# A planned Trainium2 kernel: other durations in its plan, four graph pairs in flight for five, and one output transfer for each graph

## The chip, the cores and the metric

The program runs on one core of one Trainium2 chip. The metric is the device time of one execution in microseconds, and less is better. Three runs of the kernel before took 3004.53, 3000.09 and 3002.74 us, a median of 3002.74 us.

## What is computed

The input is 64 graphs of 256 nodes with 256 features and a 0/1 adjacency of 256 x 256, all in float32. Two layers follow each other. Layer 0 is a graph attention layer used twice in a row, a layernorm, and a feed-forward block with ReLU. Layer 1 is an attention with 8 heads of 32 features, in which adjacency values pick the value projection, a layernorm, and a feed-forward block with GELU.

```python
# layer 0
def _gat(h, adj, W, a, out_features):
    Wh = jnp.matmul(h, W)
    e = leaky_relu(Wh @ a[:out_features] + swapaxes(Wh @ a[out_features:], 1, 2), 0.2)
    att = softmax(where(adj > 0, e, NEG), axis=1)
    return jnp.matmul(att, Wh)
h = _gat(_gat(x, adj, W1, a1), adj, W2, a2)
h = _layernorm(x + h)
x = _layernorm(h + relu(h @ w_ff1 + b_ff1) @ w_ff2 + b_ff2)
# layer 1
scores = einsum('bhid,bhjd->bhij', q, k) / sqrt(dh)
attn = softmax(scores, axis=-1)
for r in range(R):                       # adj holds 0 and 1 here
    out = out + einsum('bhij,bhjd->bhid', attn * (adj == r)[:, None], v_r)
x = _ln(src + out.reshape(Bb, Nn, Dm) @ Wo + bo)
return _ln(x + gelu(x @ W1 + b1) @ W2 + b2)
```

## The kernel before

The work goes by pairs of graphs, 32 of them, numbered 0 to 31 here. For each pair the generator `whole_way` gives the matmul steps of all its stages: `gat_layers` (first, second and third GAT product, "GAT1" to "GAT3" below), `feed_forward` of layer 0, `attention`, `feed_forward` of layer 1, and the store of the rows. A step is a handful of matmuls; in front of each the generator yields what the step needs: events, an exclusive name, and a number of PSUM banks. The other engines' work, the DMAs too, is handed over with `put(engine, us, emit, *events, rank=...)`.

The order of the instructions on every engine is settled before anything runs, by `run`. It is a list scheduler with a clock for each engine. `took(us)` moves TensorE's clock by a duration that is written in the code, and `put` carries one for its piece. At each turn `run` takes the engine that can begin first. On TensorE it chooses among the steps that have been ready for `SLACK` (0.3 us) the one of the lowest degree, then the one of the oldest pair. The degree is 0 for the pair in the first half of a feed-forward, 2 for a pair in its second half (`filling`), and 1 else. On another engine it takes the piece of the lowest rank. The order in which `run` emits is the order in which each engine executes on the chip; there the engines wait on semaphores alone, so that the durations in the code change the order and nothing else.

Some things are exclusive. Only one pair at a time holds the name "gat" (GAT1 and GAT2), only one "ff" (a feed-forward from its first product to its last), only one "attention" (from the first q/k/v product to the output projection). There are 4 buffers for a pair's rows `x`, 4 for its adjacency in bytes `adj`, one `input` buffer for the adjacency and the transposed input in turn, two `yT` for transposed rows, and 8 PSUM banks. `whole_way` asks for the loads of the next pair when it begins.

How many pairs are in flight is the last argument of `run`, called `together`. `run` adds 1 to it for the weights' own generator `reliefs`, which leaves after the start. In the kernel before that line stands twice:

```python
        going, ways = [[besides, *next(besides)]], iter(ways)
        together += 1
        ...
        together += 1
        while True:
            while len(going) < together and (way := next(ways, None)) is not None:
                going.append([way, *next(way)])
```

With `run(reliefs(), ..., 4)` five pairs are in flight. A new pair enters when the oldest generator has ended, which is at the last matmul step of its second feed-forward.

TensorE works in two shapes. Nearly all products are made by strips of 32 columns, four matmuls side by side (128 rows x 32 columns, by `by_strips`, line 113, and lines 960 and 963 in `products`). The four `scores` steps of a pair (line 929) contract over 32 rows and are made in the other shape, 32 rows x 128 columns. The steps of the attention stand in this order: the products for q, k and v with scores 0 and 1 among them (`b_.p4`, scores 0, `b_.p3`, scores 1), then products 0, scores 2, products 1, scores 3, products 2, products 3, and the output projection `into_rows`.

`layernorm` centres rows on VectorE (line 654) and scales them there (line 657). `transposed` brings rows into `yT` by a 32 x 32 transposition on VectorE, a store to DRAM (`home`, line 683) and four gathers for each graph (line 689), all on the queue of SyncE. The finished rows of a pair are stored by one transfer of 512 KB on the same queue (line 1097).

Of the kernel before, what the change touches and what calls it, by code (L numbers as in the profile page):

```python
# [18 lines left out]
P = 128  # L19
# [8 lines left out]
SEVEN = ()  # L28
SLACK = 0.3
START = {"tensor": 8.5, "vector": 8.0, "scalar": 4.0, "gpsimd": 0.0, "sync": 32.0}  # L30
# [3 lines left out]
def two_layers(ctx: ExitStack, tc: tile.TileContext, t: dict, out: bass.AP, flag: bass.AP):  # L34
# [114 lines left out]
    alone, filling = {}, []  # L149
# [81 lines left out]
    def run(besides, ways, together):  # L231

        going, ways = [[besides, *next(besides)]], iter(ways)
        together += 1
        def degree(g):
            if g[0] in filling:
                return 2
            return 0 if "ff" in (g[2] or ()) or alone.get("ff") is g[0] else 1  # L240

        together += 1
        while True:
            while len(going) < together and (way := next(ways, None)) is not None:
                going.append([way, *next(way)])
            first = []
            for engine, pieces in waiting.items():
                times = [(at, n) for n, p in enumerate(pieces) if (at := begins(p["ready"], p["needs"])) is not None]
                if times:
                    first.append((max(min(times)[0], clock[engine]), engine, times))  # L250
            times = []
            for n, (way, events, name, banks, *more) in enumerate(going):
                if all(alone.get(n) in (None, way) for n in name or ()) and all(e.time is not None for e in events):
                    at = begins(max([e.time for e in events], default=0.0), "bank" if banks else None, banks)
                    for needs in more:
                        at = None if at is None else begins(at, needs)
                    if at is not None:
                        times.append((at, n))
            if times:
                first.append((max(min(times)[0], clock["tensor"]), "tensor", times))  # L260
            if not first:
                assert not going
                return
            now, engine, times = min(first)
            able = [n for at, n in times if at <= now]
            clock[engine] = now
            if engine == "tensor":
                sure = [n for at, n in times if at <= now - SLACK]
                g = going[min(sure, key=lambda n: (going[n][0] is besides, degree(going[n]), n))
                          if sure else min(times)[1]]  # L270
                alone.update((name, g[0]) for name in g[2] or ())
                takes("bank", g[3])
                for needs in g[4:]:
                    takes(needs)
                step = next(g[0], None)
                if step is None:
                    together -= g[0] is besides
                    going.remove(g)
                else:
                    g[1:] = step  # L280
            else:
                piece = waiting[engine].pop(min(able, key=lambda n: (waiting[engine][n]["rank"], waiting[engine][n]["first"]["ready"])))
                takes(piece["needs"])
                if piece["function"] and piece["function"] != table[0]:
                    table[0] = piece["function"]
                    clock[engine] += 1.3
                piece["emit"]()
                clock[engine] += piece["us"]
                end = clock[engine] + piece["lag"]
                if piece["kb"]:  # L290
                    moved[0] = max(moved[0], clock[engine]) + piece["kb"] / 380.0
                    end = moved[0] + piece["lag"]
                frees_at(end, piece["frees"])
                happens(piece["event"], end)
            keep_order()
# [8 lines left out]
    def load(pair, at=None):  # L304
# [29 lines left out]
        def in_bytes(there):  # L334
            return put("vector", 1.35, largest, put("scalar", 1.2, small_adj, there, needs="adj", rank=2), rank=2)
# [51 lines left out]
    class Second:  # L387


        def __init__(self, b, name, *events):  # L390
            self.b, self.name, self.there, self.read = b, name, [], []
            for n in range(3):
                self.there.append(put("vector", 0.34, lambda n=n: self.add(n), *events, rank=0, needs=None if n else name))
# [10 lines left out]
        def read_by_second(self, event):  # L404
            self.read.append(event)
            if len(self.read) == 2:
                put("vector", 0.34, lambda: self.add(3), self.there[2], *self.read, rank=0, event=self.there[3])
# [7 lines left out]
    class Blocks:  # L415
# [17 lines left out]
        def add(self, c, h, bank, *events, frees=()):  # L433
            def add():
                nc.vector.tensor_tensor(self.target(c, h), self.bank[bank], self.target(c, h), ALU.add)  # L435
            there = put("vector", 0.6, add, *events, rank=-1, frees=frees)
# [41 lines left out]
    def addends(y, there, at, layer, pair):  # L478
# [20 lines left out]
        there = put("scalar", 0.6, exps, *there, rank=0, function="exp")  # L499
# [28 lines left out]
        there = put("vector", 0.2, turn, there, rank=0)  # L528
# [3 lines left out]
    def gat_weights(y, at, at_home, ratio, there, to, b):  # L532
# [20 lines left out]
        there = put("vector", 0.95, lambda: weigh(0), *there, rank=b / 2, needs="e")  # L553
        there = put("vector", 1.13, lambda: weigh(1), there, rank=b / 2, frees=["rows"] * b)
        return of, put_each("scalar", 0.4, [lambda j=j: scale(j) for j in range(2)], there, rank=0)

    def gat_layers(pair, to, loads):
# [3 lines left out]
        def evacuated(to, k, wide, ps):  # L561
            return put("scalar", 0.3, lambda: nc.scalar.activation(to[:, k, :wide], ps[:, :wide], AF.Copy),
                       took(0.88), frees=["bank"])
# [45 lines left out]
    def add_rows(y, p, b, *events):  # L609
# [12 lines left out]
        return of, put_each("vector", 0.44, [lambda j=j: add(j) for j in range(2)], *events, frees=["bank"])  # L622

    def means(y, b, *events):
# [8 lines left out]
        return of, put_each("scalar", 0.54, [lambda j=j: mean(j) for j in range(2)], *events)  # L633

    def layernorm(r, gb, b, added, *events):
# [23 lines left out]
        there = put_each("scalar", 0.54, [lambda j=j: square(j) for j in range(2)], there, rank=0)  # L659
        centred = put_each("vector", 0.34, [lambda j=j: centre(j) for j in range(2)], there)  # L660
        there = put("gpsimd", 1.2, root, there, rank=0)
        return put_each("vector", 0.34, [lambda j=j: scale(j) for j in range(2)], there, centred, *events)
# [5 lines left out]
    def transposed(y, ready, to, b, pair, stage):  # L668
# [23 lines left out]
        there = put("vector", 0.62, turn, ready, needs="yb")  # L692
# [25 lines left out]
    def feed_forward(y, normal, w, func, relieved, gb, pair, stage):  # L718
# [11 lines left out]
        def slabs(t):  # L730
# [11 lines left out]
            def copy(c, h, event):  # L742
                return put("scalar", 0.5, lambda: nc.scalar.activation(target(c, h), blocks.bank["x"], AF.Copy), event, rank=-1)  # L743

            def activate(c, h, event, of=None, frees=()):
                for n in range(2):
# [3 lines left out]
                        to, source, func, bias=b1[:, m:m + 1]), event, rank=h - 1, function=kind,  # L750
# [9 lines left out]
        for step in (a.p1, b.p1, a.p2, a.p6, b.p2, b.p6, a.p5, a.p7, b.p7, b.p5, a.p4, b.p4, a.p3):  # L760
            yield from step()
# [28 lines left out]
    def by_seven(y, normal, f, evacuated, w2, w2_there, last):  # L790
# [21 lines left out]
        def add(to, of, us, *events, frees=()):  # L812
            return put("vector", us, lambda: nc.vector.tensor_tensor(to, of, to, ALU.add), *events, rank=-1, frees=frees)

        def combine(to, a, b, op, *events):
            return put("vector", 1.14, lambda: nc.vector.tensor_tensor(to, a, b, op), *events, rank=0)
# [40 lines left out]
    def attention(y, normal, pair, all_adj):  # L857
# [13 lines left out]
        there = put("scalar", 0.52, lambda: in_one_piece(0), normal[0], needs="yTa")  # L871
        there = put("scalar", 0.52, lambda: in_one_piece(1), there, normal[1], frees=["yT"])
# [27 lines left out]
        def with_bias_qk(c, b, event, frees=()):  # L900
            def copy(n):
                nc.scalar.activation(target_qk(c, b)[:, n], of_qk.bank["x"][:, n], AF.Identity, bias=bqk[:, n, c:c + 1])  # L902
            return [put("scalar", 0.4, lambda n=n: copy(n), event, rank=-1, frees=list(frees) * n) for n in range(2)][1]

        def with_bias_v(r, b, event, frees=()):
# [3 lines left out]
            return put("vector", 0.6, copy, event, rank=-1, frees=frees)  # L909
# [11 lines left out]
        def scores(n):  # L921
            b, c = divmod(n, KC)
            yield [ready["qk", c, b]], None, HQ
# [7 lines left out]
            there = took(1.13)  # L931
# [12 lines left out]
            def halves(q):  # L944
# [3 lines left out]
            there = [put_each("scalar", 0.48, [lambda q=q, k=k: weight(q, k) for k in range(2)], there, rank=0, function="exp",  # L948
                              needs="a", frees=["bank"] * 2) for q in range(HQ // 2)]
            masked.append([put("vector", 1.14, lambda q=q: mask(q), there[q], rank=0, needs="m") for q in range(HQ // 2)] +  # L950
                          [put("vector", 0.61, lambda q=q: halves(q), there[q], rank=0, needs="h") for q in range(HQ // 2)])

        def products(n):
# [10 lines left out]
            there = took(2.34)  # L964
# [16 lines left out]
            there = put("vector", 1.3, invert, there, rank=0)  # L981
            put("scalar", 0.4, check, there, rank=3)
            return put("vector", 0.34, lambda: nc.vector.tensor_tensor(to, po[:, :N], s, ALU.mult), there, rank=0, frees=["bank", "h"])
# [10 lines left out]
        a_, b_ = of_qk, of_v  # L994
        for step in (a_.p1, b_.p1, a_.p2, a_.p6, b_.p2, a_.p5, b_.p6, a_.p7, b_.p5, a_.p4, b_.p7, a_.p3, b_.p4, lambda: scores(0), b_.p3, lambda: scores(1)):
            yield from step()
        frees_at(clock["tensor"], ["yTa", "sums_yTa"])
        divided = []
        for n in range(4):
            yield [*masked[n], ready["v", 0, n // 2], ready["v", 1, n // 2]], None, 1  # L1000
            divided.append(products(n))
            if n < 2:
                yield from scores(n + 2)
# [85 lines left out]
    def whole_way(pair):  # L1089
        to, loads = loaded.pop(pair)  # L1090
        if pair + 1 < NPAIR and pair + 1 not in loaded:
# [5 lines left out]
        put("sync", 0.4, lambda: nc.sync.dma_start(  # L1097
            out[2 * pair:2 * pair + 2].rearrange("b (c p) d -> p (b c) d", p=P), to["x"]),
            normal[0], normal[1], rank=2, lag=1.8, kb=512, frees=["x"])

    run(reliefs(), (whole_way(pair) for pair in range(NPAIR)), 4)


# [442 lines left out]
```

## Time and profile before

| | |
|---|---|
| runs of the kernel | 3004.53, 3000.09, 3002.74 us |
| median | 3002.74 us |
| the profiled execution's own time | 3002.45 us |
| its span (first to last instruction) | 3000.6 us |
| granted TensorE clock, mean | 0.996 |
| TensorE busy | 2962.5 us |
| VectorE busy | 2308.1 us |
| ScalarE busy | 1789.2 us |
| GpSimd busy | 293.3 us |
| DMA queue of SyncE, share of 16 engines | 21.2% |

In the profile PE is TensorE's matmul, PEld its weight load, DVE VectorE, ACT ScalarE, POOL GpSimd, SP SyncE and SPq its queue of issues. `L113` is line 113 of the kernel. A line of the timeline gives the start and the length in us, the engine, the source line, the operation, `out<-in` by the program's names, the tile shape as rows*columns, and how many records are merged. A float32 matmul leaves two records, so that four matmuls side by side over 256 columns are 8 records. The modelled end of a matmul lies after the start of the next one, so that durations of steps are read here from start to start.

### The profile page before, as it was taken

To read this page: it belongs to the slowest core of one execution; us is meant where nothing else is said; L and a number is where in the kernel's file an instruction comes from. 1 tells how busy PE (TensorE), PEld (TensorE's weight loads), DVE (VectorE), ACT (ScalarE), POOL (GpSimd) and SP (SyncE) were. 2 spreads that over 40 slices of the span, in tenths; PEclk is the share of its full clock that TensorE was granted. 3 is DMA by queue.
4 is the path that set the end of the run, shared out by engine and by line. 5 is a ranking of instruction groups with operands and counts; after the bars stand their busy time and mean duration, and the time that the engine had idled before them with its cause. 6 is when DMAs were issued, how large, how long until landed. Compare 5 with 4: busy or idle time off the path is not lost. (4 is left out here: it accounts for less than half of the span.)

```text
span 3000.6 us, 122479 instructions
## 1 busy us (share of the span) xinstructions
PE 2962.5 (99%) x53778; PEld 1766.1 (59%) x53778; DVE 2308.1 (77%) x5865; ACT 1789.2 (60%) x4644; POOL 293.3 (10%) x518
## 2 busy tenths in 40 slices
PE   7999999999999999999999999999999999999998
PEld 4655555555555555555555555555556555565665
DVE  5787875888668887588976888768886788867775
ACT  4555565665656566556665566555666565664554
POOL 0000010000101011000110001101010001100001
PEclk8999999999999999999999999999999999999999
DMA  5221231112321123121231212311232121321100
GB/s 178 80 72 52 65 110 63 52 59 66 108 65 55 55 72 119 52 69 38 92 103 55 62 51 89 99 52 59 65 97 76 59 65 53 100 74 49 39 10 24
DMA packets 211420, 210.22 MB, mean 70 GB/s; under 512 B 22336, under 2 KB 170432, under 8 KB 210880
## 3 DMA queue, kind: packets, MB, share of 16 engines
q1 hardware_dynamic: 210464, 202.06, 21.2%
q8 instruction: 424, 6.95, 1.0%
q14 instruction: 116, 0.95, 0.1%
q10 hardware_dynamic: 416, 0.26, 0.0%
HBM read 137.51 MB, written 64.73 MB: 67 GB/s over the span
## 5 line engine op out<-in xcount | busy, mean ns | idle before, releaser
L113 PE MATMUL ps<-w_L_gnn_W,ff 128*32 128x256 f32 x8192 | 470.7, 380 | 1.3 <-ACT ff L749 1.3
L113 PE MATMUL ps<-w_L_gnn_w_ff,ff 128*32 128x256 f32 x8192 | 470.7, 379 | 0.0
L113 PEld LDWEIGHTS ps<-w_L_gnn_W,ff 128*32 128x32 f32 x8192 | 260.1, 110 | 186.5 <-issue 13.6
L113 PEld LDWEIGHTS ps<-w_L_gnn_w_ff,ff 128*32 128x32 f32 x8192 | 265.1, 110 | 177.5 <-issue 3.6
L938 ACT ACTIVATE a<-ps 128x512 f32<-128x512 f32 x512 | 265.5, 600 | 170.3 <-PE ps L929 153.4
L435 DVE TENSOR_TENSOR ff<-ps,ff 128x512 f32<-128x512 f32 x384 | 262.3, 684 | 118.1 <-PE ps L113 89.6
L650 POOL TENSOR_SCALAR rstd<-squares 128x2 f32<-128x2 f32 x256 | 90.8, 355 | 2679.6 <-ACT unread L645 2678.3
L645 ACT ACTIVATE unread<-x,less 128x256 f32<-128x256 f32 x512 | 259.3, 506 | 130.1 <-DVE less L620 103.7
L942 DVE TENSOR_TENSOR m<-a,adj 128x1024 f32<-128x1024 f32 x256 | 310.7, 1214 | 23.9 <-ACT a L938 23.0
L113 PE MATMUL ps<-yT,w_L_gnn_W1p 128*32 128x256 f32 x5120 | 310.0, 379 | 0.8 <-ACT ff L743 0.3
L113 PE MATMUL ps<-yT,w_L_gnn_w_ff1p 128*32 128x256 f32 x5120 | 306.7, 379 | 0.0
L617 DVE SCALAR_TENSOR_TENSOR x<-ps,x 128x256 f32<-128x256 f32 x512 | 197.3, 417 | 136.0 <-PE ps L113 133.0
L743 ACT ACTIVATE ff<-ps 128x512 f32<-128x512 f32 x384 | 224.2, 588 | 112.9 <-PE ps L113 111.3
L113 PE MATMUL ps<-xw,e 128*32 128x258 f32 (+1 forms) x4096 | 242.7, 386 | 11.9 <-ACT xw L551 11.9
L551 ACT ACTIVATE xw<-xw,rs 128x258 f32<-128x258 f32 (+1 forms) x256 | 118.0, 504 | 201.2 <-DVE rs L547 201.1
L113 PEld LDWEIGHTS ps<-yT,w_L_gnn_W1p 128*32 128x32 f32 x5120 | 165.6, 110 | 112.9 <-ACT ff L743 4.9
L113 PEld LDWEIGHTS ps<-yT,w_L_gnn_w_ff1p 128*32 128x32 f32 x5120 | 165.5, 110 | 110.9 <-issue 2.3
L902 ACT ACTIVATE qk<-ps,bqk 128x256 f32<-128x256 f32 x256 | 107.1, 469 | 190.0 <-PE ps L113 189.8
L749 ACT ACTIVATE ff<-ff,c_L_gnn_b_ff 128x256 f32<-128x256 f32 x384 | 175.5, 503 | 50.5 <-DVE ff L435 47.8
L651 POOL TENSOR_TENSOR rstd<-rstd,mhalf 128x2 f32<-128x2 f32 x256 | 201.8, 788 | 21.3
L113 PEld LDWEIGHTS ps<-xw,e 128*32 128x32 f32 x4096 | 133.8, 112 | 104.6 <-ACT xw L551 14.1
L749 ACT ACTIVATE ff<-ff,c_L_gnn_b 128x256 f32<-128x256 f32 x384 | 175.9, 502 | 28.6 <-DVE ff L435 26.0
(126 smaller groups left out, 4748.2 us busy)
## 6 DMA issues: line engine op xcount, KB each, us to landing
home<-yb SPq DMA_DIRECT2D x182, 256.0 KB, 2.1
yT<-home SPq DMA_DIRECT2D x728, 64.0 KB, 2.1
rows<-row SPq DMA_DIRECT2D x60, 512.0 KB, 3.9
input<-in_xT SPq DMA_DIRECT2D x32, 512.0 KB, 4.0
x<-in_x SPq DMA_DIRECT2D x32, 512.0 KB, 3.9
out<-x SPq DMA_DIRECT2D x32, 512.0 KB, 3.0
input<-in_adjT SPq DMA_DIRECT2D x30, 512.0 KB, 4.0
v<-in_adjT SPq DMA_DIRECT2D x2, 512.0 KB, 7.5
```

The lines of the kernel that those rows point to most:

```text
L113: nc.tensor.matmul(to[at:at + DH], lhsT=lhsT[:, at:at + DH], rhs=rhs, **flags)
L435: nc.vector.tensor_tensor(self.target(c, h), self.bank[bank], self.target(c, h), ALU.add)
L551: nc.scalar.activation(y[:, k, :at], y[:, k, :at], AF.Copy, scale=of["rs"][:, j:j + 1])
L617: nc.vector.scalar_tensor_tensor(row, p[:, j * D:(j + 1) * D], 1.0, row, op0=ALU.mult, op1=ALU.add, accum_out=of["less"][:, j:j + 1])
L645: nc.scalar.activation(unread, rows[j], AF.Square, bias=of["less"][:, j:j + 1], accum_out=squares[:, j:j + 1])
L650: nc.gpsimd.tensor_scalar(rstd, squares, 1.0 / D, EPS, ALU.mult, ALU.add)
L651: nc.gpsimd.tensor_tensor(rstd, rstd, mhalf[:, :2], ALU.pow)
L743: return put("scalar", 0.5, lambda: nc.scalar.activation(target(c, h), blocks.bank["x"], AF.Copy), event, rank=-1)
L749: evacuated[h][m] = put("scalar", 0.4, lambda m=m, to=to, source=source: nc.scalar.activation(to, source, func, bias=b1[:, m:m + 1]), even ...
L902: nc.scalar.activation(target_qk(c, b)[:, n], of_qk.bank["x"][:, n], AF.Identity, bias=bqk[:, n, c:c + 1])
L938: nc.scalar.activation(a[n][q][:, k], ps[2 * q + k], AF.Exp)
L942: nc.vector.tensor_tensor(m[n][q], a[n][q], adj, ALU.mult)
```

## The change

The durations in the code change in four places: the scores' step from 1.13 to 0.97 us, the products' step from 2.34 to 2.17 us, and the layernorm's centring and scaling from 0.34 to 0.4 us each. `run` learns of a shape: a scores step carries the name "rows", and where the chosen step's shape differs from the one before, TensorE's clock in the plan moves by 0.1 us. The degrees move into a table `DEGREE`, with entries for a scores step and for one "after" another; the ranks of `put` move into a table `RANK`; the orders of steps in the feed-forward, in q/k/v and in the rest of the attention move into `FIRST`, `QKV` and `GROUPS`. One of the two lines `together += 1` goes. The one store of a pair's rows becomes two, one for each graph: the first waits for its own graph's layernorm alone, the second gives the buffer `x` free.

```diff
+SHAPES = ("rows",)
+FLIGHT = 4
+RANK = {'adj': 2, 'second': 0, 'blocks': -1, 'exps': 0, ..., 'rows': 1, 'means': 1, 'centre': 1, 'scale': 1, 'turn': 1, 'piece': 1, 'evac': 1}
+DEGREE = {"first": 0, "gat": 1, "attention": 1, "fill": 2, "rows": 1, "after": 1}
+GROUPS = (([0], []), ([], [2]), ([1], []), ([], [3]), ([2], []), ([3], []))
+FIRST = ("a1", "b1", "a2", "a6", "b2", "b6", "a5", "a7", "b7", "b5", "a4", "b4", "a3")
+QKV = ("a1", "b1", "a2", "a6", "b2", "a5", "b6", "a7", "b5", "a4", "b7", "a3", "b4", "s0", "b3", "s1")
...
         going, ways = [[besides, *next(besides)]], iter(ways)
-        together += 1
+        def shape(g):
+            return next((n for n in g[2] or () if n in SHAPES), None)
+
         def degree(g):
-            if g[0] in filling:
-                return 2
-            return 0 if "ff" in (g[2] or ()) or alone.get("ff") is g[0] else 1
+            kind = ("fill" if g[0] in filling else "first" if "ff" in (g[2] or ()) or alone.get("ff") is g[0] else
+                    "attention" if "attention" in (g[2] or ()) or alone.get("attention") is g[0] else "gat")
+            return DEGREE["after" if shaped[0] and shape(g) else shape(g) or kind]
 
         together += 1
         while True:
...
-                alone.update((name, g[0]) for name in g[2] or ())
+                alone.update((name, g[0]) for name in g[2] or () if name not in SHAPES)
+                if shape(g) != shaped[0]:
+                    clock[engine] += 0.1
+                    shaped[0] = shape(g)
...
-        centred = put_each("vector", 0.34, [lambda j=j: centre(j) for j in range(2)], there)
+        centred = put_each("vector", 0.4, [lambda j=j: centre(j) for j in range(2)], there, rank=RANK["centre"])
...
-        return put_each("vector", 0.34, [lambda j=j: scale(j) for j in range(2)], there, centred, *events)
+        return put_each("vector", 0.4, [lambda j=j: scale(j) for j in range(2)], there, centred, *events, rank=RANK["scale"])
...
         def scores(n):
             b, c = divmod(n, KC)
-            yield [ready["qk", c, b]], None, HQ
...
-            there = took(1.13)
+            there = took(0.97)
...
-            there = took(2.34)
+            there = took(2.17)
...
+        def narrow(groups, later):
+            yield ([e for n in groups for e in (*masked[n], ready["v", 0, n // 2], ready["v", 1, n // 2])] +
+                   [ready["qk", n % KC, n // KC] for n in later],
+                   ["rows"] * bool(later), len(groups) + HQ * len(later))
+            divided.extend(products(n) for n in groups)
+            for n in later:
+                scores(n)
...
-        for n in range(4):
-            yield [*masked[n], ready["v", 0, n // 2], ready["v", 1, n // 2]], None, 1
-            divided.append(products(n))
-            if n < 2:
-                yield from scores(n + 2)
+        for groups, later in GROUPS:
+            yield from narrow(groups, later)
...
-        put("sync", 0.4, lambda: nc.sync.dma_start(
-            out[2 * pair:2 * pair + 2].rearrange("b (c p) d -> p (b c) d", p=P), to["x"]),
-            normal[0], normal[1], rank=2, lag=1.8, kb=512, frees=["x"])
-
-    run(reliefs(), (whole_way(pair) for pair in range(NPAIR)), 4)
+        there = []
+        for b in range(2):
+            there.append(put("sync", 0.4, lambda b=b: nc.sync.dma_start(
+                out[2 * pair + b].rearrange("(c p) d -> p c d", p=P), to["x"][:, of_graph(b), :]),
+                normal[b], *there, rank=2, lag=1.8, kb=256, frees=["x"] * b))
+
+    run(reliefs(), (whole_way(pair) for pair in range(NPAIR)), FLIGHT)
```

## The prediction

> **What bounds the kernel now.** I read the page first, then TensorE's waits, then the busy time by stretches, and last the timelines of TensorE and of SyncE's queue. The page:
>
> ```profile
> span 3000.6 us, 122479 instructions
> ...
> PE 2962.5 (99%) x53778; PEld 1766.1 (59%) x53778; DVE 2308.1 (77%) x5865; ACT 1789.2 (60%) x4644; POOL 293.3 (10%) x518
> ...
> PEclk8999999999999999999999999999999999999999
> ...
> home<-yb SPq DMA_DIRECT2D x182, 256.0 KB, 2.1
> ...
> out<-x SPq DMA_DIRECT2D x32, 512.0 KB, 3.0
> ```
>
> TensorE is busy 99% at full clock, and is idle for 3000.6 - 2962.5 = 38.1 us in all. Where, the windows tell (first and second number: length and TensorE's busy time):
>
> ```profile
> 78.00:217.00 139.00, 137.81 (x2532) 82.30 (x2528) 111.23 (x299) 80.07 (x221) 12.62 (x24) 1.00 0.24 78
> 217.00:430.00 213.00, 209.84 (x3808) 123.75 (x3804) 173.92 (x438) 131.59 (x345) 23.38 (x40) 1.00 0.22 68
> ...
> 1522.00:1888.00 366.00, 365.41 (x6664) 217.42 (x6657) 287.46 (x729) 223.23 (x579) 36.35 (x64) 1.00 0.23 72
> ...
> 2622.00:2991.00 369.00, 369.00 (x6834) 222.46 (x6823) 257.16 (x622) 205.97 (x532) 32.62 (x61) 1.00 0.12 38
> ```
>
> Before 78 us it is idle for 19.3 us (78 less 58.67 busy), after 2991 us for 9.5 (9.60 less 0.08). What lies between, 38.1 - 19.3 - 9.5 = 9.3 us, is all that an order of the steady work can still gain. 2622 to 2991 has none at all. The table of TensorE's waits agrees: its longest is at the start, and from 430 us on it lists 4.0 us in sum, the longest 0.7.
>
> ```profile
> PE ps L113 <- ACT xw L551: 11.9, 4, 8.5
> ```
>
> The timeline of TensorE gives the steps that the change renames or moves:
>
> ```profile
> 43.83 6.55 PE L113 MATMUL ps<-xw,e 128*32 128x256 f32 x64 [8.50 <-ACT xw L551]
> ...
> 1779.51 1.91 PE L113 MATMUL ps<-w_L_gnn_W,ff 128*32 128x256 f32 x32
> ...
> 1814.83 1.94 PE L113 MATMUL ps<-w,input 128*32 128x260 f32 x32
> ...
> 1868.67 3.64 PE L113 MATMUL ps<-xw,e 128*32 128x256 f32 x64
> ...
> 1889.24 1.05 PE L113 MATMUL ps<-yT,w_L_gnn_w_ff1p 128*32 128x256 f32 x16
> ...
> 2355.78 1.05 PE L113 MATMUL ps<-wv,yTa 128*32 128x256 f32 x16
> 2356.75 1.15 PE L929 MATMUL ps<-qk 32*128 32x256 f32 x16
> 2357.83 1.07 PE L113 MATMUL ps<-wv,yTa 128*32 128x256 f32 x16
> ...
> 2372.86 1.07 PE L960 MATMUL ps<-a,v 128*32 128x256 f32 x16
> ...
> 2375.04 1.91 PE L113 MATMUL ps<-w_L_gnn_w_ff,ff 128*32 128x256 f32 x32
> ```
>
> **Shape and durations.** Sixteen records in the ordinary shape go by in 0.86 us (1855.67 to 1856.53). Before a scores step they take 0.97, and the scores step takes 1.08 to the next start: a lone scores step costs 0.33 us more than its matmuls, 128 of them 42 us. None of this leaves. A scores step could save by standing behind another one, but the plan has no such place: in `QKV` and `GROUPS` a q/k/v or products step lies between any two of a pair, and "attention" keeps the other pairs out. `DEGREE` gives "after", "rows", "attention" and "gat" the same 1, `RANK` repeats the old ranks, and the step lists repeat the old order. So the stated preference decides nothing; the 0.1 us is added after the choice.
>
> What changes is the plan's clock. A scores step with the two changes of shape is 0.97 + 0.1 + 0.1 = 1.17 us there, for 1.13 before and 0.86 + 0.33 = 1.19 measured. Products go from 2.34 to 2.17; the row at 2372.86 to 2375.04 has 2.18. TensorE's plan is shorter by 4 x 0.17 - 4 x 0.04 = 0.5 us a pair. Centring and scaling go from 0.34 to 0.40 where their groups have 0.47 us: 32 pieces a pair, 1.9 us more on VectorE's plan. All three come nearer to the chip. None is work: the chip's cost is zero as long as the new order keeps TensorE fed. Its bounds: no steady idle at all is -9.3 us; the rate of the worst stretch (217 to 430: 3.16 in 213 us, 1.5%) over all 2913 us from 78 to 2991 is 43 us, +34. I take 0, since five stretches from 430 to 2254 lie within 0.2 to 1.5 us and are nearest to the bulk of the work, and the two shares of the edit (truer durations, fewer choices) point in opposite directions.
>
> **Four pairs for five.** This is the weightiest part. Now a fifth pair does GAT1 and GAT2 ahead (7 us of TensorE) and then stands still, because its rows need the `x` of the oldest pair. Pair 20's first GAT steps run at 1676 to 1705, its GAT3 only at 1806, after pair 16's store at 1793.86 and the load at 1797.10. With four, pair 20 enters where pair 16 makes its last step (1779.51 above), so those 7 us move behind it, and GAT3 comes later. Does its feed-forward still come in time? From the first GAT1 matmul to the last of GAT3 pair 21 takes 1814.83 to 1872.13, 57 us. The transposition after pair 20's GAT3, which ends at 1812:
>
> ```profile
> 1815.40 0.34 SPq L683 DMA_DIRECT2D home<-yb  x1
> ...
> 1822.01 0.46 SPq L683 DMA_DIRECT2D home<-yb  x1
> 1822.56 6.61 SPq L689 DMA_DIRECT2D yT<-home  x8
> ```
>
> The last gather is issued at 1829.2 and lands 2.1 later, so 19 us after GAT3. Entering to ready is 57 + 19 = 76 us. Pair 20 would be ready at 1781 + 76 = 1857, and its feed-forward begins at 1889.24 now: 32 us to spare. In the same way: pair 4, entering at 314 where pair 0 ends, is ready at 390 and due at 423 (33 to spare); pair 21 1928 for 1952 (24); pair 22 1965 for 1995 (30); pair 23 2028 for 2053 (25); the last pair, 31, 2761 for 2777 (16). The loads are ahead of it: adjacency and transposed input of pair 21 are issued 1821.52 and 1831.43 in the trace, 10 us apart, and the new order asks for them one entry (37 to 71 us) early. So I cost the move at nothing; what covers it is the feed-forward of the pairs that finish, whose second half can go at any time. Without that cover a pair would cost up to 76 - 26 = 50 us once (a feed-forward alone takes 25.9 us: 2964.77 to 2990.67). What is late next if a pair comes late is the exclusive "ff".
>
> A hole would cost more than its length: after the wait of 8.50 us the GAT3 steps at 43.83 take 6.55 us, and the same 64 records 3.64 us at 1868.67, so 2.9 us on top; after waits up to 1.1 us nothing of the kind shows. The Trainium skill ("TensorE: Matmul & The Clock Gate", Part 1) puts the point at about 3.4 us of idle time. By it only a hole longer than any wait after 78 us would pay this; no run here shows that limit.
>
> **The stores.** 32 transfers of 512 KB become 64 of 256 KB. Inside, nothing waits for them but the next load of rows; SyncE's queue gets 32 more issues of 0.40 us, 13 us in 3000. The first store is due some 7 us before the second (the two last additions of rows stand at 2984.23 and 2991.14), and the second when the one store is due now. Behind them in the queue stand the load of rows and the `home` stores and gathers of other pairs, on which a later feed-forward waits; none is held longer than now. At the end only the second graph's store counts. It is issued at 2995.75, right after the last scaling, and lands 3.0 later. At 256 KB: `home<-yb` lands in 2.1, but has longer runs; a gather of 64 KB also takes 2.1, so much is fixed. Bounds -0.9 and 0; I take -0.7, nearer to the row of the same size. The Trainium skill speaks against small transfers ("DMA: Bandwidth & Descriptors", Bandwidth: batch to 1 MiB and more). [...]
>
> **The sum.** The profiled execution took 3002.45 us, 1.85 outside its span and 0.29 below the median of the runs. 3002.45 + 0 (shape) + 0 (order) + 0 (GAT moved) - 0.7 = 3001.75, and with the 0.29 about 3002.0 us.
>
> **The rivals.** Slower: the fifth pair was the reserve. While feed-forwards follow each other and no attention runs (1850 to 1976 in this trace), GAT steps are the only other work; if entering to ready takes over some 100 us instead of 76, because the newest pair is served last, TensorE waits at each change of "ff". It decides from about 25 us of lateness on. For it: the only stretch with much idle time is 217 to 430, where pairs begin to replace each other. Against: 78 to 217 and 2695 to 2991 run with four or fewer pairs and lose 1.2 and 0.0 us. With half of the worst stretch's excess everywhere it is +17, 3019 us; with all of it 3036.
>
> Faster: truer durations and no early GAT work remove the steady waits. More than 0.2% (6 us) needs 5.3 of the 9.3 us beside the 0.7; about 2995 us, never below 2992. Against: even the rates of the two best stretches together (1.2 us in 508) leave 6.8 us in 2913.
>
> The change does not do what it says: scores behind scores. If 64 joins came about and each saved one leaving and one entering (0.22 us), 14 us, 2988; the step order excludes it, and it has 1% inside "faster".
>
> **How the numbers follow.** 0.2% or 6 us is about what a measurement of this kernel can tell from no change. Forecast, within 6 us of 3002.7: 0.50, own range 2997 to 3008. Slower 0.36, faster 0.14. The range 2993 to 3024 leaves out the upper part of the slower case and next to nothing below.
>
> **What would show it.** Right: GAT1 of pair 4 near 315 instead of 189; 128 lone scores steps, still 0.97 and 1.08; steady idle of 5 to 15 us; the last store landing in 2.1 to 2.6. Wrong: waits of several us in front of `ff` or `yT` steps after 314 us, a slower clock behind them, or a last pair whose stages stand alone after 2777.

## The result and the profile after

Six runs of the changed kernel took 3023.95 to 3039.08 us, with a median of 3032.27 us. Six runs of the kernel before, on the same chip, took 3000.09 to 3004.53 us, with a median of 3003.18 us. The ratio is 1.0099, with a 95% interval from 1.0081 to 1.0117. The change makes the kernel 1% slower. The prediction was 3002.0 us, "within 0.2%", with a range up to 3024. The profiled execution is the fastest of the six, 3023.95 us.

First the page of the changed kernel, the same rows as before the change:

```profile
span 3022.2 us, 122598 instructions
...
PE 2965.5 (98%) x53778; PEld 1770.2 (59%) x53778; DVE 2308.2 (76%) x5865; ACT 1769.4 (59%) x4632; POOL 268.6 (9%) x518
```

The span is 21.6 us longer. TensorE's busy time is only 3.0 us more, so 18.6 us of it are idle time: 3022.2 - 2965.5 = 56.7 us, where it was 38.1. The windows say where. They are cut at stages like those shown before, and the first and second number are the length and TensorE's busy time:

```profile
78.00:217.00 139.00, 136.85 (x2536) 81.91 (x2528) 108.79 (x292) 81.31 (x223) 14.81 (x28) 1.00 0.24 75
217.00:430.00 213.00, 212.87 (x3868) 126.51 (x3860) 166.62 (x400) 129.64 (x336) 17.81 (x32) 1.00 0.21 67
...
814.00:1188.00 374.00, 367.76 (x6672) 217.41 (x6668) 287.71 (x732) 220.66 (x578) 33.64 (x65) 1.00 0.21 70
...
1556.00:1924.00 368.00, 364.74 (x6644) 216.96 (x6640) 286.57 (x726) 219.40 (x576) 33.18 (x64) 1.00 0.22 71
...
2662.00:3013.00 351.00, 348.02 (x6406) 208.94 (x6398) 252.55 (x617) 197.50 (x511) 30.05 (x58) 1.00 0.12 39
```

The stretch 217 to 430, the worst one before, is now full. Behind it the pairs come in waves of four, some 370 us each; the two waves shown (third and fourth row) lose 6.24 and 3.26 us, and the six from 430 to 2662 lose 21.4 together. The last stretch, which was without any idle time, loses 2.98. From 78 us to 2991 the kernel before was idle for 9.3 us; this one is idle for 26.7 us from 78 to 3013. The table of TensorE's waits from 78 us on names the releaser, with the sum, the number and the longest:

```profile
PE ps L120 <- ACT ff L755: 21.0, 14, 4.3
PE ps L120 <- ACT xw L563: 4.2, 6, 1.4
PE ps L120 <- DVE qk L447: 1.0, 1, 1.0
PE ps L120 <- DVE ff L447: 0.3, 1, 0.3
```

Line numbers have shifted: L755 is the copy of a feed-forward's first products out of PSUM on ScalarE (L743 before), L563 the scaling of GAT weights there (L551 before). The copy's entry was 4.7 us in 7 waits, the longest 1.1. It is now 21.0 in 14, the longest 4.3. The scores steps still stand alone, and cost what they did (0.97 us to the scores step, 1.08 from it):

```profile
2018.02 1.05 PE L120 MATMUL ps<-wv,yTa 128*32 128x256 f32 x16
2018.99 1.15 PE L941 MATMUL ps<-qk 32*128 32x256 f32 x16
2020.07 1.07 PE L120 MATMUL ps<-wv,yTa 128*32 128x256 f32 x16
```

Why the copy is late, the longest of these waits shows. This is the chain of waits from 874 us on, in order of time (start, length, what):

```profile
875.13 5.67 DMA home<-yb
...
882.12 3.29 DMA yT<-home
...
885.52 0.63 ACT yTa L881
886.15 1.60 ACT xw L563 x4
887.75 0.49 ACT ff L755
```

And this is the timeline of the same stretch (start, length, engine, line):

```profile
874.60 0.43 SPq L537 DMA_DIRECT2D rows<-row  x1
...
875.13 0.38 SPq L695 DMA_DIRECT2D home<-yb  x1
...
881.16 2.77 PE L120 MATMUL ps<-yT,w_L_gnn_w_ff1p 128*32 128x256 f32 x48
...
885.52 0.63 ACT L881 ACTIVATE yTa<-yT 128x512 f32<-128x512 f32 x1 [8.70 <-DMA yT<-home]
886.06 1.69 ACT L563 ACTIVATE xw<-xw,rs 128x256 f32<-128x256 f32 x4
...
887.65 1.06 ACT L755 ACTIVATE ff<-ps 128x512 f32<-128x512 f32 x2
...
888.28 1.94 PE L120 MATMUL ps<-sums_yT,w_L_gnn_w_ff1p 128*32 128x256 f32 x16 [4.34 <-ACT ff L755]
```

Read it from the bottom. TensorE has made the first three products of a feed-forward (881.16, 48 records) and can't go on until ScalarE has copied one. ScalarE sits idle for 8.70 us in front of a copy that belongs to another pair (`yTa`, for the attention), because the plan put that one first and an engine executes its instructions in the order written. That copy waits for a gather, the gather for the store `home`, and the store was issued 0.5 us behind the spread of a GAT's rows to all partitions (`rows<-row`, 512 KB). It landed 5.67 us after its issue. Of the 182 `home` stores 7 are issued right behind a spread; their median to landing is 4.4 us (4.0 to 5.7), that of the other 175 is 2.15. Behind each of the seven, 10 to 14 us after its issue, ends one wait of TensorE for the copy (0.4 to 4.3 us). These seven waits make 14.7 of the 26.5 us.

Behind the 4.34 us come 32 records in 3.23 us (888.28 to 891.51), for 1.73 at full clock. The same is seen after the waits that end at 514.70 and 2733.63; the three cost 1.5, 1.7 and 1.7 us on top of the waits, and they are counted as busy.

The change has four parts: pairs in flight, durations with the shape, ranks and orders in tables, stores. The experiments separate the first, the second and the fourth. The third writes the old values into names; no run separates it from the second.

### The profile page after: what moved, and what is told of

Same layout as the page of the kernel before. It is cut to its first block, busy times and chain, and to the rows that moved or that the text cites. A ratio compares the mean times of both kernels' runs of the same rounds, so it can differ in the third digit from the quotient of the medians.

```text
span 3022.2 us, 122598 instructions
## 1 busy us (share of the span) xinstructions
PE 2965.5 (98%) x53778; PEld 1770.2 (59%) x53778; DVE 2308.2 (76%) x5865; ACT 1769.4 (59%) x4632; POOL 268.6 (9%) x518
## 3 DMA queue, kind: packets, MB, share of 16 engines
q1 hardware_dynamic: 210976, 202.06, 20.7%
## 4 chain that ended last, share of the span: by engine, by line
PE 81%; DMA 7%; DVE 7%; SPq 3%; ACT 2%; issue 1%; POOL 0%; DVEq 0%; POOLq 0%; ACTq 0%
PE ps L120 67%; PE ps L972 7%; PE ps L941 4%; DMA home<-yb 4%; SPq L701 2%; PE ps L975 2%; DMA rows<-row 1%; DVE e L556 1%; ACT xw L563 1%; DVE e L554 1%; DVE x L669 1%; DMA yT<-home 1%; DVE x L629 1%; DVE x L666 1%; DMA row<-blocks 1%
## 5 line engine op out<-in xcount | busy, mean ns | idle before, releaser
L120 PEld LDWEIGHTS ps<-w_L_gnn_W,ff 128*32 128x32 f32 x8192 | 262.5, 110 | 181.5 <-issue 11.3
L662 POOL TENSOR_SCALAR rstd<-squares 128x2 f32<-128x2 f32 x256 | 75.8, 296 | 2726.3 <-ACT unread L657 2724.7
L755 ACT ACTIVATE ff<-ps 128x512 f32<-128x512 f32 x384 | 224.3, 589 | 78.1 <-PE ps L120 76.1
L563 ACT ACTIVATE xw<-xw,rs 128x258 f32<-128x258 f32 (+1 forms) x256 | 117.9, 502 | 135.6 <-DVE rs L559 135.6
L663 POOL TENSOR_TENSOR rstd<-rstd,mhalf 128x2 f32<-128x2 f32 x256 | 192.2, 751 | 21.3
```

Source lines behind the costliest of these rows:

```text
L120: nc.tensor.matmul(to[at:at + DH], lhsT=lhsT[:, at:at + DH], rhs=rhs, **flags)
L563: nc.scalar.activation(y[:, k, :at], y[:, k, :at], AF.Copy, scale=of["rs"][:, j:j + 1])
L663: nc.gpsimd.tensor_tensor(rstd, rstd, mhalf[:, :2], ALU.pow)
```

## The experiments

**One part undone: five pairs in flight again.** All else is as in the changed kernel.

```diff
-FLIGHT = 4
+FLIGHT = 5
```

> The changed kernel with five pairs in flight again and everything else of the change kept. If the lost fifth pair is the cause, it goes back to 2995 to 3007 us, TensorE idle in steady state at 5 to 14 us, no wait of TensorE over 2 us after 78 us. If the new durations and the shape in the plan are the cause, or the two stores, it stays at 3020 to 3040 us.

2993.19 us, ratio 0.9957 [0.9941, 0.9974] to the kernel before. From 78 to 2980 us the waits are nearly gone:

```profile
PE ps L120 <- ACT ff L755: 2.9, 4, 2.1
PE ps L120 <- DVE ff L447: 0.4, 1, 0.4
PE ps L120 <- DVE qk L447: 0.3, 1, 0.3
```

The loss is in the number of pairs alone; what else changes is a gain of 0.4%. Six `home` stores stand right behind a spread here as well (median 4.3 us to landing), so the late transfers are there with five pairs and don't hurt. What differs is what TensorE has to do meanwhile. This is the stretch behind the latest of the six, which landed 5.9 us after its issue. ScalarE stands here too, for 3.33 us, in front of the copy `yTa` (from the timelines of SyncE's queue, TensorE and ScalarE):

```profile
1337.05 0.33 SPq L537 DMA_DIRECT2D rows<-row  x1
1337.66 0.32 SPq L695 DMA_DIRECT2D home<-yb  x1
...
1339.27 1.15 PE L941 MATMUL ps<-qk 32*128 32x256 f32 x16
1340.34 3.66 PE L120 MATMUL ps<-w_L_gnn_w_ff,ff 128*32 128x256 f32 x64
1343.82 1.05 PE L972 MATMUL ps<-a,v 128*32 128x256 f32 x16
...
1348.65 0.63 ACT L881 ACTIVATE yTa<-yT 128x512 f32<-128x512 f32 x1 [3.33 <-DMA yT<-home]
```

In the 14 us behind each of the six, TensorE makes scores and products of an attention and the second half of a feed-forward, and is never idle. In the 14 us behind each of the seven of the changed kernel it has products of feed-forwards alone (in the longest one, the rest of one and the beginning of the next), and stands once. The kernel before had five such stores, landing in 4.1 to 4.3 us, all beside an attention.

**One part alone: four pairs with the old durations.**

```diff
         going, ways = [[besides, *next(besides)]], iter(ways)
-        together += 1
```

> The kernel before with the one line taken out, four pairs in flight, old durations, one store. If the lost fifth pair is the cause, 3015 to 3040 us with waits of TensorE for the feed-forward's copy on ScalarE. If the durations are the cause, 3000 to 3006 us as before. If the truer durations softened the loss, over 3040 us.

3032.93 us, ratio 1.0092 [1.0073, 1.0111]. With the old durations four pairs cost 27 us. The waits sum up to more than 33 us and stand mostly in front of the same two kinds of steps, in other shares:

```profile
PE ps L113 <- ACT xw L550: 18.9, 12, 2.6
PE ps L113 <- ACT ff L742: 10.3, 7, 2.6
PE ps L113 <- DVE qk L434: 3.1, 2, 1.7
```

No `home` store stands right behind a spread in this order. Four gathers do, 14 times; they land in a median of 3.8 us (2.7 to 5.5), all gathers in 2.0. The longest wait shows that they do the same harm through another engine:

```profile
2359.28 0.38 SPq L524 DMA_DIRECT2D rows<-row  x1
2359.70 1.85 SPq L688 DMA_DIRECT2D yT<-home  x4
...
2365.55 0.42 DVE L401 TENSOR_TENSOR sums_yT<-yT 128x256 f32<-128x256 f32 x1 [3.90 <-DMA yT<-home]
2365.90 0.48 DVE L541 SCALAR_TENSOR_TENSOR e<-rows,ratio 128x256 f32<-128x256 f32 x1
...
2368.40 0.91 ACT L550 ACTIVATE xw<-xw,rs 128x256 f32<-128x256 f32 x2 [6.96 <-DVE rs L546]
...
2368.96 1.29 PE L113 MATMUL ps<-xw,e 128*32 128x256 f32 x20 [2.63 <-ACT xw L550]
```

VectorE stands for 3.90 us in front of an addition that needs the last gather (4.36 us to landing). The GAT weights that TensorE needs next are queued behind that addition.

**Durations and stores apart.** `five_and_one_store` is the changed kernel with `FLIGHT = 5` and the old store of 512 KB put back; `five_old_two_stores` is the kernel before with the new stores:

```diff
+        there = []
+        for b in range(2):
+            there.append(put("sync", 0.4, lambda b=b: nc.sync.dma_start(
+                out[2 * pair + b].rearrange("(c p) d -> p c d", p=P), to["x"][:, of_graph(b), :]),
+                normal[b], *there, rank=2, lag=1.8, kb=256, frees=["x"] * b))
-        put("sync", 0.4, ..., normal[0], normal[1], rank=2, lag=1.8, kb=512, frees=["x"])
```

> Five in flight and the single store of 512 KB: what is left of the change is the durations and the shape. If these are neutral, 2996 to 3007 us; if they are the cause, 3020 to 3040. Against the run with five in flight and two stores it tells the price of the stores: about 0.8 us at the end if only the last landing counts, nothing inside.

> The kernel before with two stores of 256 KB for the one of 512, five in flight, old durations. If the stores matter at the end alone, 0.8 us less than before; if their own place in the order frees SyncE's queue, 3 to 6 us less; if they clog it, more than before.

The first took 2998.58 us, ratio 0.9977 [0.9967, 0.9986]: with five pairs the new durations (with the shape and the new names) are a gain of 0.2%, some 7 us. With four pairs no gain of theirs shows: 1.0092 without them, 1.0099 with them and the new stores. The second took 2999.30 us, ratio 0.9992 [0.9983, 1.0002]: the stores alone are worth 2 us or nothing. On top of the new durations they are worth more (2998.58 to 2993.19, on one chip).

**Three pairs in flight.**

> The changed kernel with three in flight. If each pair less uncovers more of the plan's errors, 3060 us and more, with single waits well over 4 us and a lower clock behind them. If four were the edge only by the place of one transfer, 3020 to 3045 us.

3163.07 us, ratio 1.0530 [1.0510, 1.0550]. Here the loss is of another kind. TensorE waits for gathers, and the granted clock is 0.975:

```profile
PE ps L120 <- DMA yT<-home: 108.8, 11, 13.0
```

Once in each wave of three pairs, ten times, TensorE stands for 10 to 13 us in front of the first product of a feed-forward of layer 1, because its rows have not been gathered. That is the hand-over at "ff" that the prediction's rival told of; in the changed kernel no listed wait after 78 us is of this kind.

**Is it the spread? The same order, a smaller transfer.** Both kernels have four pairs and one order on every engine, and keep one buffer for `rows`. The second spreads the rows to 32 partitions instead of 128; the other 96 hold a constant, so that its GAT weights are others.

```diff
-            nc.sync.dma_start(rows.rearrange("p q n c -> p (q n c)"),
-                              at_home["row"].rearrange("j q c -> (j q c)").partition_broadcast(P))
+            nc.sync.dma_start(rows.rearrange("p q n c -> p (q n c)")[:32],
+                              at_home["row"].rearrange("j q c -> (j q c)").partition_broadcast(32))
```

> The control of the run with the narrow transfer: one buffer set at the start, the whole transfer of 512 KB, every engine's order as in the changed kernel. Both theories: as the changed kernel, 3022 to 3040 us, with TensorE's waits after 78 us at 20 to 40 us.

> The changed kernel, four in flight, every engine's order kept. The DMA that spreads the GAT row writes 32 partitions instead of 128, 128 KB for 512; this leaves out the rows of the other 96 partitions, which keep what was there (one buffer that is set once at the start holds them all). If the waits come from this transfer, which is slower than the plan says and holds up the home store behind it, the store lands in about 2 us, TensorE's waits after 78 us fall from 24 us to under 10, and the time to 2998 to 3012 us. If four pairs hold too little work whatever the transfers take, or another queue is late, it stays within 5 us of the run with the same buffer and the whole transfer.

With the full spread 3022.70 us, ratio 1.0073 [1.0056, 1.0089]; with the small one 3002.00 us, ratio 1.0002 [0.9993, 1.0012]. They differ by 20.7 us. The waits of the first kernel, and the landing of its `rows`:

```profile
PE ps L122 <- ACT ff L757: 20.0, 13, 4.3
PE ps L122 <- ACT xw L565: 5.4, 7, 1.3
...
DMA to landing us min/median/max: 3.4/3.9/5.5
```

and of the second:

```profile
PE ps L122 <- ACT ff L757: 9.2, 11, 1.7
PE ps L122 <- DVE qk L449: 1.0, 1, 1.0
...
PE ps L122 <- ACT xw L565: 0.3, 1, 0.3
...
DMA to landing us min/median/max: 2.2/2.4/4.8
```

The spread lands 1.5 us earlier, the `home` stores right behind it have a median of 2.6 us for 4.5 (three of the seven still take 3.5 to 4.7), and the sum of waits falls from 26 to 11 us. Since nothing else differs in what is executed or in what order, the landing of this one transfer, with those behind it, makes 20.7 us. Some is left: by the ratios (1.0002 and 0.9957) this is still 13 us above five pairs. And the test has a limit: the small spread lands in 2.4 us where the plan expects 3.85, so it also lends the plan slack that could cover lateness of another origin on the same path.

**The same with the old durations.** `only_four_in_flight` with the small spread:

> The kernel before with the one line taken out (four in flight, old durations, one store) and the GAT row spread over 32 partitions instead of 128; the rows of the other 96 partitions are left out. No home store stands right behind a spread in that order. If the slow spread is what a late plan trips over with old durations too, 3000 to 3015 us and TensorE's waits after 78 us down from 33 us to under 15. If the spread matters only through the home store behind it, it stays at 3025 to 3040 us.

3011.27 us, ratio 1.0024 [1.0013, 1.0036], for 1.0092 with the full one. The four gathers behind the spread now land in a median of 2.1 us for 3.8. Here, too, the spread makes most of the loss, so the cause does not depend on the new durations, nor on a `home` store right behind a spread.

**Can the plan be told?** The plan prices the spread at 512 KB on the DMA engines (512 / 380 = 1.35 us) and 2.5 us of `lag`. The total of 3.85 us is right (4.0 measured), but only 1.35 of it keep the next transfer waiting in the plan, while the `home` store behind it measures 2.2 us more than another. So the price is raised to 1500 (1500 / 380 = 3.95 us), with four pairs and with five:

```diff
-        return at_home, ratio, [put("sync", 0.4, spread, there, rank=0, lag=2.5, kb=512, needs="rows")]
+        return at_home, ratio, [put("sync", 0.4, spread, there, rank=0, lag=2.5, kb=1500, needs="rows")]
```

> The changed kernel, four in flight, with one figure of the plan altered: the DMA that spreads the GAT row over all partitions holds the plan's DMA time for 3.9 us (kb=1500) where it held it for 1.3 (kb=512). In the trace a home store issued right behind it lands 5.7 us later, not 2.2, and the next copy of the feed-forward stands on ScalarE behind work that waits for that landing. If this mispriced collision is what makes the plan's order wrong, TensorE's waits for the copy fall from 21 us to under 8 and the time to 3000 to 3015 us. If four pairs simply do not hold enough work, it stays over 3020 us.

> Five in flight and the spread priced at 3.9 us of the plan's DMA time. If the reserve pair and the truer price mend the same fault, the second brings little on top of the first: 2985 to 2995 us. If the price has a fault of its own, as one wait of 12 us at 181 us in the run with four suggests, 2995 to 3008 us.

With four pairs 3005.54 us, ratio 0.9997 [0.9987, 1.0007]. All that TensorE waits for from 78 to 2980 us is this:

```profile
PE ps L120 <- DMA home<-yb: 12.0, 1, 12.0
PE ps L941 <- DVE qk L995: 0.4, 1, 0.4
```

Behind the one long wait at 181 us it is never idle until 2992 us, but for 0.4, though 15 `home` stores stand right behind a spread there and land 4.1 to 4.7 us after their issue. So in this order four pairs do hold enough work to keep TensorE fed beside late transfers. That the old price was the fault does not follow: the edit also makes the plan expect the spread itself only after some 6.4 us, where 4.0 are measured. And the wait of 12.0 us at the start gives most of the gain back. With five pairs the price does harm: 3015.58 us, ratio 1.0043 [1.0029, 1.0058], which neither theory had expected. A wait of like length appears at the start, now for a load, and some 5 us more near the end:

```profile
PE ps L120 <- DMA input<-in_xT: 11.7, 1, 11.7
PE ps L721 <- DVE x L669: 4.9, 2, 3.0
```

**The higher price without the start.** Two variants: `kb=1500 if pair >= 4 else 512` with four pairs, and `kb=1500 if 4 <= pair < NPAIR - 4 else 512` with five.

> Four in flight, the spread priced at 3.9 us of the plan's DMA time from pair 4 on; the start keeps the old price. If the one wait of 12 us at 181 us is all that the earlier price cost, 2988 to 2996 us, no wait over 1 us after 78 us, and four pairs are then no worse than five. If four pairs hold too little work and the first price hid it by luck, 3000 us and more.

> Five in flight, the price of 3.9 us for pairs 4 to 27 alone; start and end keep the old one. With five the priced run had no wait between 193 and 2955 us, one of 12 before and some 6 after. If start and end are all it lost, 2986 to 2994 us. If a new order at the seam costs as much, 2995 to 3010.

3000.40 us, ratio 0.9987 [0.9977, 0.9996], and 3012.29 us, ratio 1.0027 [1.0018, 1.0037]. The first stands where its second case begins ("four pairs hold too little work", from 3000 us on). The 12 us are gone, but 6.2 us of idle time are back between 430 and 2650, most of it in front of a feed-forward whose rows have not been gathered:

```profile
PE ps L120 <- DMA yT<-home: 5.3, 5, 1.5
```

The second misses: it is idle for 5.4 us in the middle and for 6.1 near the end, where the price had been taken back. What a price gained in one stretch of one order was not kept when the order around it changed.

**A price with the same total.** `kb=1500` and `lag=0.1`, so that the plan expects the spread itself when it expected it before, and only the next transfer later.

> Four in flight, all pairs: the spread holds the plan's DMA time for 3.9 us and is down 0.1 us later, so that it lands 4.0 us after its issue as in the trace (4.0) and not after 6.4. If the 12 us wait at the start came from the landing priced too late, it goes: 2988 to 2996 us. If it comes from the held DMA time itself, 3000 to 3008 us.

> Five in flight with the same truer landing. If the landing was the fault of the run with five and the price, 2986 to 2995 us; if the held time is, 3008 to 3018 us as there.

With four pairs 3004.99 us, ratio 0.9997 [0.9988, 1.0007]. The wait at the start is gone, so it came from the landing that was expected too late, as the first case had it; but the time is that of the second case, as the copy's waits are partly back:

```profile
PE ps L120 <- ACT ff L755: 7.9, 10, 3.3
PE ps L120 <- ACT xw L563: 5.1, 6, 2.2
```

With five pairs 2990.55 us, ratio 0.9958 [0.9941, 0.9975]. This version and `five_in_flight` (0.9957) are faster than both kernels, and equal among themselves. The best version with four pairs has 0.9987. So with the truer price four pairs win back most of their loss, not all of it, and why not all was not tested.

## Why the prediction was wrong, point by point

**What bounds the kernel.** This was read rightly. TensorE is the bound, the idle time of 38.1 us was nearly all at the two ends, and the order could gain no more than 9.3 us. The bound was a little too narrow. The profiled span of `five_in_flight` is 9.8 us shorter than that of the kernel before, but only 3.9 of them are idle time (38.1 to 34.2) and 5.9 are busy time of TensorE (2962.5 to 2956.6), though its matmuls are the same. Whether these are gaps too short to be listed was not settled.

**Shape.** Right: 128 lone scores steps, 0.97 and 1.08 us, none joined to another.

**Durations.** Taken as 0, with bounds of -9.3 and +34. With five pairs they are -7 us, inside the bounds. That run holds the durations, the shape and the names together, and no run tells the two shares ("truer durations, fewer choices") apart.

**Four pairs for five.** This is the step that failed: "So I cost the move at nothing; what covers it is the feed-forward of the pairs that finish, whose second half can go at any time." The term measured 27 us with the old durations (3032.93 less 3005.84), and with the new ones some 40 (39 by the medians of 3032.27 and 2993.19, 43 by the ratios 1.0099 and 0.9957). Its check was right as far as it went: GAT1 of pair 4 began at 320.9 (foretold near 315), and no listed wait of TensorE after 78 us is for a gather, so no feed-forward was late for its turn. The check asked the wrong question. It compared whole stages, and asked whether each pair comes in time for "ff". The loss lies inside the stages: the first half of a feed-forward needs a copy on ScalarE after three products, ScalarE is held by another pair's transfer (8.70 us in the case shown), and in that moment TensorE needs something else that is ready. With five pairs there was such work, an attention's. With four there was none: the second half of the feed-forward before had just ended, at 881.16, and no attention ran. The transfers were taken at their medians (2.1 us for `home`). The ones that matter stand right behind a spread: 7 of 182 stores with 4.4 us here, the gathers with 3.8 in `only_four_in_flight`. The trace of the kernel before had five such stores, at 4.1 to 4.3.

**The stores.** The last one's landing was put between 2.1 and 2.6 us, for 3.0 before. The median of all is 2.2, but the last one took 2.7 and the last of before 3.2, so that the end gained 0.5. The 0.7 us can't be told apart in the total time: alone, the stores measured -2.4 us with an interval that holds no change.

**The slower rival** had the right cause, "the fifth pair was the reserve", and the right side. Its place was wrong: "TensorE waits at each change of "ff"" is what three pairs do, not the changed kernel. Its price of 17 us (3019) was too low against 29 measured, the upper one of 34 (3036) was near. Its evidence was misread, too: the stretch 217 to 430, taken as the sign for it, lost 0.13 us with four pairs. The evidence against it, that 78 to 217 and the last 300 us run with four or fewer pairs at almost no loss, was no evidence on the middle, where 21.4 of the 26.7 us are lost.

**The faster rival** is what the change does with five pairs (0.9957). The argument against it misread the windows: the "two best stretches together (1.2 us in 508)" are 2622 to 2991, without any idle time, and 78 to 217, which at 1.19 us in 139 is the second worst of the nine.

**The slow clock** behind a hole was foreseen, with 2.9 us for each, and dismissed as no hole was expected. It came three times, at 1.5 to 1.7 us, 4.9 us in all.

**What stays open.** Why the two kernels with the late price fell short was not settled. Some 12 of the changed kernel's 26.5 us of waits do not end behind one of the seven stores. The small spread lowers them too (from 11.3 to 4.4 us, those behind the seven from 14.7 to 6.6), but they were not followed back one by one. The six runs of the changed kernel lie 15 us apart, those of before 4.4. Its waits hang on when transfers land, which could explain it, but that was not tested.

## What to carry to other kernels

In an order that is planned ahead, the number of items in flight buys slack against durations that the plan has wrong; count what is ready at the moment when an engine is held, not whether each item meets its next stage. Look for the transfers that stand right behind a large one in their queue: their landing is what a copy on an in-order engine waits for, and with it everything queued behind that copy. To see whether one transfer is the cause, shrink that transfer and keep the order of all engines; what lands earlier than planned also lends slack, so follow one wait back as well.

## What the runs showed of the hardware that was not expected

A `home` store of 256 KB issued right behind a 512 KB spread lands 4.4 us after its issue, otherwise 2.15; gathers of 64 KB right behind one take 3.8 us (`only_four_in_flight`), otherwise 2.0. Over the whole span the DMA engines are far from full (20.7% of 16 engines' span in the changed kernel).

The half clock came behind shorter waits than the one of 8.50 us that the prediction had. Waits of 2.91, 4.34 and 2.52 us (ending at 514.70, 888.28 and 2733.63) are followed by a granted clock of 0.50 or 0.51 over 3.4 us, those of 1.88 and 1.92 us (1627.47 and 1995.55) are not. There is no sharp point: in `four_kept_buffer` a wait of 2.16 us ending at 209.81 is followed by a granted clock of 0.72 over the next 6 us, and one of the same length ending at 1628.08 by 1.00; in `only_four_in_flight` 2.58 us ending at 781.35 is followed by 1.00 as well, and so is in `only_four_narrow` 3.79 us ending at 1148.04. The Trainium skill ("TensorE: Matmul & The Clock Gate", Part 1) has the clock halved after an idle window of about 3.4 us that runs free of the work. The waits here that paid it start at two thirds of that (2.16 us), and one a little longer (3.79) did not pay it, so the length that it gives is no sharp bound for this kernel. That the same length has both outcomes agrees with a window that runs free.
